# An FFN's first layer as seven products of quarters (Strassen) over blocks of 1024 tokens, in a fused gated block

## The chip, the core and the metric

The kernel runs on one core of a Trainium2 chip. The core has a matrix engine (TensorE, "PE" in the profile; its weight loads are listed apart as "PEld"), VectorE ("DVE"), ScalarE ("ACT"), GpSimd ("POOL") and an engine that here only issues transfers ("SP"). Each engine works through its own list of instructions in order; engines wait for one another by semaphores. The metric is the device time of one execution in microseconds (us). "Median" is over the runs shown.

## The reference

2048 tokens of 512 numbers go through two gated residual steps. All numbers are float32.

```python
# step 1: each token belongs to one of 4 experts, by its id; ctx[e] is 512 x 512
h = layernorm(x)
g = silu(h @ ctx[e].T)
u = h @ ctx[e].T                # the same matrix is used for gate, up and down
x = x + tanh(g_xattn) * ((g * u) @ ctx[e].T)    # e: the token's expert

# step 2: a dense FFN; its results are added up into 8 rows
xr = layernorm(x)
probs = softmax(xr @ wr.T)      # 8 routes
top2, idx = top_k(probs, 2)
gates = top2 / top2.sum()
h = silu(xr @ w1.T)
h = silu(h @ w3.T)
h = h @ w2.T
out = zeros_like(x)
for k in range(2):
    out[idx[:, k]] += gates[:, k] * h
x = x + tanh(g_ffn) * out
```

Since idx is at most 7, only rows 0 to 7 of `out` are not zero. The gated sum can so be taken before the last product with w2, over all tokens.

## The kernel before, in words

**Sorting.** Tokens are sorted by expert on the chip. They fill 17 "slots" of 128 rows: 13 slots of whole tiles of one expert (numbers 0 to NF - 1 = 12), and four "packed" slots (13 to 16, written NF to NF + 3) whose four groups of 32 rows can have different experts. A whole slot needs one matrix of 1 MB, a packed slot four. `from_row` and `to_row` hold, for each slot, which rows of x it reads and writes.

**One slot.** POOL gathers its rows (`gather`, an indirect transfer). DVE takes the mean off (`centre`: bn_stats, bn_aggr, subtract). TensorE transposes the tile into `tp_a` (`turn_in`), and ACT copies it to `hT`. TensorE multiplies it with the expert's matrix `m` into `z` (`up`); ACT makes g = silu(z), and DVE multiplies g by z. TensorE transposes g (`turn_mid`, `tp_g`), ACT copies it to `gT`, and TensorE multiplies with the same matrix into `y` (`down`). DVE adds y to x; POOL scatters the new rows to the output (an indirect transfer). DVE normalises them for the FFN (`norms`: bn_stats, an inverse root in nine small steps, together with that of a later slot's first norm). TensorE transposes the result (`turn_out`, `tp_f`), and ACT copies it into `hT2`, a block's input with tokens along the columns. For a packed slot ACT makes four copies, at column positions read from the table `first`.

**The main loop.** It is written out by hand as a software pipeline over `order`, the list of slots. Turn i does up(i), turn_in(i+1), centre(i+2), gather(i+3) and load(i+3), down(i-1), turn_out(i-2), norms(i-1), turn_mid(i). Here "slot i" in a turn means the i-th of `order`. TensorE's list in one turn is thus: z (four matmuls), tp_a, y (four matmuls), tp_f, tp_g. The order in which the code is written is the order on every engine: nothing is rescheduled.

**FFN work as filler.** `ffn(b)` is a generator over a block of 512 tokens. `step()` runs it up to its next `yield`, and is called twice in each turn. It becomes available when the last slot of its block has been through turn_out. Its parts are: four products `u` (L582; 128 columns of w1 each, all 512 tokens, four row chunks of 128 summed in one PSUM bank), each followed by a Silu on ACT into `s1`; the route logits `lg` (16 small products in groups of 32 columns), which DVE transposes and from which `route` makes the gates; four products `v` with w3, each followed by a Silu into `s2`; and four small products that add gate times s2 into `acc`. What is left when the loop ends runs as a tail with nothing beside it. In the last block the end is cut finer (`add_turned`, `finish`, `out_product`), and the 8 rows are written.

**Buffers.** The expert matrices rotate through eight buffers (`mp`), the x tiles through five (`xp`). PSUM has eight banks: four for products of all kinds (`ps_mm`), three for transposes (`ps_tp`), one for `acc`. A buffer is reused when its last reader is done. The instruction that fills it waits for that, and so does all that stands behind it on its engine or queue. SP's queue carries all loads of matrices and weights in the order of the code; POOL's queue carries gathers and scatters; ACT's and SP's carry the last stores.

**Start.** While the sort runs, TensorE does matmuls on constants (`busy`). ACT computes tanh of the two gates first; its first Silu is that of g of slot 0. The weights w1, wr, w3 and w2 are loaded behind the first matrices.

## Time and profile before

| | |
|---|---|
| median of 3 runs | 288.35 us (288.25 to 288.72) |
| the profiled execution | 287.71 us, of which 286.0 are the span from the first to the last instruction |
| TensorE busy | 275.3 us (96% of the span), granted clock 1.0 |
| DVE, ACT, POOL busy | 128.4, 63.9 and 38.9 us |
| products z, y (each 232 records) | 61.8 and 61.5 us busy |
| products u, v (128 and 136 records) | 57.1 and 57.3 us busy |
| transfers | 42.5 MB, 149 GB/s over the span; about 392 GB/s from 29 to 64 us |

All times below are of the profiled execution, from the start of its span. A float32 matmul instruction appears as two records. TensorE's records overlap, since ends are modelled, so its durations are best read from one start to the next. A line of the timeline gives start, duration, engine, line and operation, output and inputs, and in brackets the idle time before it and what ended that. A line of the groups gives the number of records, the busy time, the mean of one in ns, and the idle time before them.

### The profile page before, as it was taken

To read this page: it belongs to the slowest core of one execution; us is meant where nothing else is said; L and a number is where in the kernel's file an instruction comes from. 1 tells how busy PE (TensorE), PEld (TensorE's weight loads), DVE (VectorE), ACT (ScalarE), POOL (GpSimd) and SP (SyncE) were. 2 spreads that over 40 slices of the span, in tenths; PEclk is the share of its full clock that TensorE was granted. 3 is DMA by queue.
4 is the path that set the end of the run, shared out by engine and by line. 5 is a ranking of instruction groups with operands and counts; after the bars stand their busy time and mean duration, and the time that the engine had idled before them with its cause. 6 is when DMAs were issued, how large, how long until landed. Compare 5 with 4: busy or idle time off the path is not lost.

```text
span 286.0 us, 3546 instructions
## 1 busy us (share of the span) xinstructions
PE 275.3 (96%) x1189; PEld 128.2 (45%) x1189; DVE 128.4 (45%) x572; ACT 63.9 (22%) x122; POOL 38.9 (14%) x62
## 2 busy tenths in 40 slices
PE   4889999999999999999999999999999999999994
PEld 1444455544435444534444544444343454344463
DVE  5488868764617751608260775160543330001300
ACT  2032233122222222221222222222221121111120
POOL 5420122221111111111111111010110100000000
PEclk9999999999999999999999999999999999999999
DMA  0677999994614169513269614053100000000000
GB/s 1 206 272 264 395 392 390 390 391 176 220 37 174 52 226 398 220 39 138 82 198 386 242 54 183 0 184 143 39 0 37 13 0 1 0 0 2 0 1 2
DMA packets 20722, 42.54 MB, mean 149 GB/s; under 512 B 2143, under 2 KB 2207, under 8 KB 20704
## 3 DMA queue, kind: packets, MB, share of 16 engines
q1 hardware_dynamic: 17664, 33.66, 32.2%
q0 software_dynamic: 2720, 8.65, 8.3%
q8 instruction: 9, 0.15, 0.2%
q14 instruction: 9, 0.07, 0.1%
q10 hardware_dynamic: 320, 0.01, 0.1%
HBM read 38.10 MB, written 4.47 MB: 149 GB/s over the span
## 4 chain that ended last, share of the span: by engine, by line
PE 91%; DVE 4%; DMA 3%; issue 1%; ACT 0%; POOL 0%; DVEq 0%
PE y L448 21%; PE u L582 19%; PE v L609 19%; PE z L448 19%; PE tp_f L375 3%; PE tp_g L375 2%; PE tp_a L375 2%; DMA x<-in_x_dram,from_row 2%; PE acc L621 2%; PE lg L595 1%; DMA idt<-in_ids_dram 1%; PE accT L631 1%; PE o L685 0%; ACT hT L512 0%; PE tok L266 0%
## 5 line engine op out<-in xcount | busy, mean ns | idle before, releaser
L448 PE MATMUL z<-m,hT 128*32 128x512 f32 (+1 forms) x232 | 61.8, 595 | 0.2 <-ACT hT L423 0.2
L448 PE MATMUL y<-m,gT 128*32 128x512 f32 (+1 forms) x232 | 61.5, 594 | 0.0
L582 PE MATMUL u<-hT,w 128*128 128x512 f32 x128 | 57.1, 595 | 0.5 <-ACT hT L512 0.5
L609 PE MATMUL v<-w,s 128*128 128x512 f32 (+1 forms) x136 | 57.3, 570 | 0.0
L462 DVE SCALAR_TENSOR_TENSOR g<-z,rs_a,g 128x512 f32<-128x512 f32 x17 | 12.8, 750 | 61.5 <-ACT g L461 61.5
L448 PEld LDWEIGHTS z<-m,hT 128*32 128x32 f32 (+1 forms) x232 | 22.9, 146 | 30.7 <-issue 29.6
L609 PEld LDWEIGHTS v<-w,s 128*128 128x128 f32 x136 | 24.9, 190 | 25.5 <-issue 24.9
L582 PEld LDWEIGHTS u<-hT,w 128*128 128x128 f32 x128 | 23.4, 190 | 27.1 <-issue 26.2
L448 PEld LDWEIGHTS y<-m,gT 128*32 128x32 f32 (+1 forms) x232 | 22.5, 146 | 27.9 <-issue 27.9
L477 POOL DMA_INDIRECT out_dram<-x,to_row x17 | 17.2, 1010 | 109.8 <-DVE x L476 108.6
L384 POOL DMA_INDIRECT x<-in_x_dram,from_row x17 | 16.6, 978 | 73.5 <-issue 25.4
L476 DVE SCALAR_TENSOR_TENSOR x<-y,tg,x 128x512 f32<-128x512 f32 x17 | 12.7, 750 | 20.9 <-PE y L448 20.9
L461 ACT ACTIVATE g<-z,rs_a 128x512 f32<-128x512 f32 x17 | 11.7, 687 | 38.4 <-PE z L448 32.7
L589 ACT ACTIVATE s<-u 128x512 f32<-128x512 f32 x16 | 9.6, 597 | 47.2 <-PE u L582 47.2
L617 ACT ACTIVATE s<-v 128x512 f32<-128x512 f32 (+1 forms) x17 | 9.7, 572 | 41.3 <-PE v L609 41.3
L554 DVE STREAM_TRANSPOSE lt<-lg 128x128 f32<-128x128 f32 x4 | 1.3, 317 | 37.2 <-PE lg L595 37.2
L512 ACT COPY hT<-tp_f 128x512 f32<-128x512 f32 x13 | 7.6, 586 | 42.7 <-PE tp_f L375 42.7
L335 DVE BATCH_NORM_STATS2 st_a<-x 128x6 f32<-128x512 f32 x16 | 11.0, 686 | 5.3 <-DMA x<-in_x_dram,from_row 5.3
L375 PEld LDWEIGHTS tp_f<-ident,h_f 128*128 128x128 f32 x68 | 8.2, 141 | 10.2 <-issue 10.2
L335 DVE BATCH_NORM_STATS2 st_f<-x 128x6 f32<-128x512 f32 x17 | 11.8, 695 | 0.6
L375 PEld LDWEIGHTS tp_a<-ident,h_a 128*128 128x128 f32 x64 | 7.7, 141 | 9.5 <-issue 7.8
L375 PEld LDWEIGHTS tp_g<-ident,g 128*128 128x128 f32 x68 | 8.1, 141 | 7.6 <-issue 6.3
(139 smaller groups left out, 201.1 us busy)
## 6 DMA issues: line engine op xcount, KB each, us to landing
m<-in_ctxT_dram SPq DMA_DIRECT2D x29, 1024.0 KB
w<-in_w1T_dram SPq DMA_DIRECT2D x1, 1024.0 KB
w<-in_w3T_dram SPq DMA_DIRECT2D x1, 1024.0 KB
w<-in_w2T_dram SPq DMA_DIRECT2D x1, 1024.0 KB
x<-in_x_dram,from_row POOLq DMA_INDIRECT x17, 5.7
out_dram<-x,to_row POOLq DMA_INDIRECT x17, 5.8
wr<-in_wrT_dram SPq DMA_DIRECT2D x1, 64.0 KB
x_first<-out_dram SPq DMA_DIRECT2D x4, 4.0 KB
```

The lines of the kernel that those rows point to most:

```text
L335: nc.vector.bn_stats(st, xt)
L375: nc.tensor.transpose(tp[:, k * P : (k + 1) * P], h[:, k * P : (k + 1) * P], ident)
L384: nc.gpsimd.indirect_dma_start(out=xt, out_offset=None, in_=x, in_offset=bass.IndirectOffsetOnAxis(ap=from_row[:, p : p + 1], axis=0),)
L448: nc.tensor.matmul(out_ps[i * n : (i + 1) * n, :], lhs[:, k * P + i * n : k * P + (i + 1) * n], m[:, k, :], start=(k == 0), stop=(k == KC ...
L461: nc.scalar.activation(g, z, AF.Silu, scale=rs)
L462: nc.vector.scalar_tensor_tensor(g, z, rs, g, ALU.mult, ALU.mult)
L476: nc.vector.scalar_tensor_tensor(xt, y, tg[:, 0:1], xt, ALU.mult, ALU.add)
L477: nc.gpsimd.indirect_dma_start(out=out, out_offset=bass.IndirectOffsetOnAxis(ap=to_row[:, p : p + 1], axis=0), in_=xt, in_offset=None, bou ...
L582: nc.tensor.matmul(u, w1[:, k, m * P : (m + 1) * P], hT[:, k, 0:TB], start=(k == 0), stop=(k == KC - 1),)
L589: nc.scalar.activation(s1[:, m, :], u, AF.Silu)
L609: nc.tensor.matmul(v, s1[:, k, t * P : (t + 1) * P], w3[:, k, c0 : c0 + n], start=(k == 0), stop=(k == KC - 1),)
L617: nc.scalar.activation(s2, v, AF.Silu)
```

## The change

Blocks become 1024 tokens (two instead of four). The first layer of a block, the product of w1 and hT2, is cut into quarters: w1 into A11, A12, A21, A22 (256 x 256, as stored with the input rows first), hT2 into B11, B12, B21, B22 (256 rows x 512 tokens). In place of eight products of quarters there are seven, by Strassen's scheme in Winograd's form. Four sums of w1's quarters, S1 to S4, are made once on POOL in turn 4; four sums of the block's input, T1 to T4, on DVE once the block is complete. A product of quarters is four matmul instructions: two column chunks c, two row chunks each, summed in a PSUM bank. Some products add onto the bank X that an earlier one has left, after ACT has copied the earlier state out (`kept`: c1, u2, c7); others are joined by a DVE add that writes s1 before its Silu (`active` with `other`). Those Silu are issued one step later (`catch_up`).

The logits of both halves of a block are computed when it is complete, ahead of the sums, in the banks that X will take. A block's second layer is as before, over its two halves of 512 tokens.

PSUM is shared out anew: two banks for z, y, v and Z, two for X and the logits, one for Y, two for transposes, one for acc. The matrices have seven buffers instead of eight. `hT`, `gT` and `g` have two instead of three, `s2` four instead of five. The tables of the sort lie in a pool that is closed, whose place the FFN's new tiles take. In `order` the first packed slot moves from position 7 to 6. The loads of w3 and w2 move from ahead of the loop to the end of turn 7. A Silu of the gates is put ahead of their tanh.

```diff
     assert E == 4 and G == 4
-    TB = 512
+    TB = 1024
     NB = NT // TB
-    TT = TB // P
+    HB = TB // 2
+    TT = HB // P
+    assert NB == 2 and KC == 4
     const = ctx.enter_context(tc.tile_pool(name="const", bufs=1))
-    mp = ctx.enter_context(tc.tile_pool(name="mp", bufs=8))
-    hp = ctx.enter_context(tc.tile_pool(name="hp", bufs=2))
+    mp = ctx.enter_context(tc.tile_pool(name="mp", bufs=7))
     xp = ctx.enter_context(tc.tile_pool(name="xp", bufs=5))
     work = ctx.enter_context(tc.tile_pool(name="work", bufs=3))
-    s1p = ctx.enter_context(tc.tile_pool(name="s1p", bufs=2))
     small = ctx.enter_context(tc.tile_pool(name="small", bufs=4))
-    ps_mm = ctx.enter_context(tc.tile_pool(name="ps_mm", bufs=4, space=bass.MemoryType.PSUM))
-    ps_tp = ctx.enter_context(tc.tile_pool(name="ps_tp", bufs=3, space=bass.MemoryType.PSUM))
+    ps_mm = ctx.enter_context(tc.tile_pool(name="ps_mm", bufs=2, space=bass.MemoryType.PSUM))
+    ps_x = ctx.enter_context(tc.tile_pool(name="ps_x", bufs=2, space=bass.MemoryType.PSUM))
+    ps_y = ctx.enter_context(tc.tile_pool(name="ps_y", bufs=1, space=bass.MemoryType.PSUM))
+    ps_tp = ctx.enter_context(tc.tile_pool(name="ps_tp", bufs=2, space=bass.MemoryType.PSUM))
     ps_acc = ctx.enter_context(tc.tile_pool(name="ps_acc", bufs=1, space=bass.MemoryType.PSUM))
+    positions = ExitStack()
+    pos = positions.enter_context(tc.tile_pool(name="pos", bufs=1))
+    on_the_way = {
+        "lane", "atlane12", "atlane4", "passes", "what", "place", "over", "rank_in", "incl",
+        "keep", "cum", "hot", "before", "later", "stepped", "behind",
+    }
     def ct_(shape, dtype, name):
+        if name in on_the_way:
+            return pos.tile(list(shape), dtype, tag=name, name=name)
         return const.tile(list(shape), dtype, tag=name, name=name)
...
     tg = ct_([P, 2], F32, "tg")
+    nc.scalar.activation(tg, gates, AF.Silu)
     nc.scalar.activation(tg, gates, AF.Tanh)
...
-    hT2 = {NB - 1: ct_([P, KC, TB + Q], F32, "hT2")}
+    hT2 = [ct_([P, KC, TB + (Q if b == NB - 1 else 0)], F32, f"hT2_{b}") for b in range(NB)]
+    s1 = ct_([P, KC, TB], F32, "s1")
     acc = ps_acc.tile([P, D], F32, tag="acc", name="acc")
...
-    order = [0, 1, 2, 3, 4, 5, 6, NF, 7, 8, NF + 1, 9, 10, NF + 2, 11, 12, NF + 3]
+    order = [0, 1, 2, 3, 4, 5, NF, 6, 7, 8, NF + 1, 9, 10, NF + 2, 11, 12, NF + 3]
     assert sorted(order) == list(range(NP))
...
         if p < NF:
-            b = p // TT
-            if b not in hT2:
-                hT2[b] = hp.tile([P, KC, TB], F32, tag="hT2", name=f"hT2_{b}")
-            nc.scalar.copy(hT2[b][:, :, p % TT * P : (p % TT + 1) * P], tp)
+            b, t = divmod(p, TB // P)
+            nc.scalar.copy(hT2[b][:, :, t * P : (t + 1) * P], tp)
             return
...
-    def route(b, lg):
+    def route(b, lt):
...
-        lt = small.tile([P, TT, Q], F32, tag="lt", bufs=2, name=f"lt_{b}")
-        nc.vector.transpose(lt.rearrange("p t q -> p (t q)"), lg)
         l1 = lt[:, :, 0:NR]
...
-    def ffn(b):
-        hT = hT2.pop(b)
-        s1 = s1p.tile([P, KC, TB], F32, tag="s1", name=f"s1_{b}")
-        for m in range(KC):
-            u = ps_mm.tile([P, TB], F32, tag="mm", name=f"u_{b}_{m}")
-            for k in range(KC):
+    def sums_of_w1():
+        h = D // 2
+        a11, a12 = w1[:, 0:2, 0:h], w1[:, 2:4, 0:h]
+        a21, a22 = w1[:, 0:2, h:D], w1[:, 2:4, h:D]
+        ss = [ffp.tile([P, 2, h], F32, tag=f"S{i}", name=f"S{i}") for i in range(1, 5)]
+        nc.gpsimd.tensor_add(ss[0], a21, a22)
+        nc.gpsimd.tensor_sub(ss[1], ss[0], a11)
+        nc.gpsimd.tensor_sub(ss[2], a11, a21)
+        nc.gpsimd.tensor_sub(ss[3], a12, ss[1])
+        return a11, a12, a22, ss
+    def sums_of_hT(b):
+        lgs = [logits(b, half) for half in range(2)]
+        b11, b12 = hT2[b][:, 0:2, 0:HB], hT2[b][:, 0:2, HB:TB]
+        b21, b22 = hT2[b][:, 2:4, 0:HB], hT2[b][:, 2:4, HB:TB]
+        ts = [ffp.tile([P, 2, HB], F32, tag=f"T{i}", name=f"T{i}_{b}") for i in range(1, 5)]
+        nc.vector.tensor_sub(ts[0], b12, b11)
+        lts[b] = [turned(b, half, lg) for half, lg in enumerate(lgs)]
+        nc.vector.tensor_sub(ts[1], b22, ts[0])
+        nc.vector.tensor_sub(ts[2], b22, b12)
+        nc.vector.tensor_sub(ts[3], b21, ts[1])
+        return b11, b21, b22, ts
+    def first_layer(b):
+        a11, a12, a22, (sa1, sa2, sa3, sa4) = w1_sums
+        b11, b21, b22, (t1, t2, t3, t4) = hT_sums[b]
+        xs_, c1s, u2s, ys, c7s = {}, {}, {}, {}, {}
+        late = []
+        def product(out_ps, a, bb, c, start):
+            for k in range(2):
                 nc.tensor.matmul(
-                    u,
-                    w1[:, k, m * P : (m + 1) * P],
-                    hT[:, k, 0:TB],
-                    start=(k == 0),
-                    stop=(k == KC - 1),
+                    out_ps,
+                    a[:, k, c * P : (c + 1) * P],
+                    bb[:, k, :],
+                    start=start and k == 0,
+                    stop=k == 1,
+                    skip_group_check=True,
                 )
-            nc.scalar.activation(s1[:, m, :], u, AF.Silu)
-            yield
-        lg = ps_tp.tile([P, P], F32, tag="tp", name=f"lg_{b}")
+        def kept(ps, name, c):
+            t = ffp.tile([P, HB], F32, tag=name, name=f"{name}_{b}_{c}")
+            nc.scalar.copy(t, ps)
+            return t
+        def active(m, half, ps, other=None):
+            to = s1[:, m, half * HB : (half + 1) * HB]
+            if other is not None:
+                nc.vector.tensor_add(to, ps, other)
+                late.append(to)
+            else:
+                nc.scalar.activation(to, ps, AF.Silu)
+        def catch_up():
+            for to in late:
+                nc.scalar.activation(to, to, AF.Silu)
+            late.clear()
+        def p1(c):
+            xs_[c] = ps_x.tile([P, HB], F32, tag="x", name=f"X_{b}_{c}")
+            product(xs_[c], a11, b11, c, True)
+            c1s[c] = kept(xs_[c], "c1", c)
+        def p2(c):
+            z = ps_mm.tile([P, HB], F32, tag="mm", name=f"Z_{b}_{c}")
+            product(z, a12, b21, c, True)
+            active(c, 0, z, c1s.pop(c))
+        def p6(c):
+            product(xs_[c], sa2, t2, c, False)
+            u2s[c] = kept(xs_[c], "u2", c)
+        def p7(c):
+            ys[c] = ps_y.tile([P, HB], F32, tag="y", name=f"Y_{b}_{c}")
+            product(ys[c], sa3, t3, c, True)
+            c7s[c] = kept(ys[c], "c7", c)
+        def p5(c):
+            product(xs_[c], sa1, t1, c, False)
+            active(2 + c, 1, xs_[c], c7s.pop(c))
+        def p4(c):
+            product(ys[c], a22, t4, c, False)
+            active(2 + c, 0, ys.pop(c), u2s.pop(c))
+        def p3(c):
+            product(xs_[c], sa4, b22, c, False)
+            active(c, 1, xs_.pop(c))
+        todo = [
+            (p1, 0), (p2, 0), (p1, 1), (p2, 1), (p6, 0), (p7, 0), (p5, 0),
+            (p4, 0), (p3, 0), (p6, 1), (p7, 1), (p5, 1), (p4, 1), (p3, 1),
+        ]
+        for i, (f, c) in enumerate(todo):
+            f(c)
+            if i % 2 == 1:
+                yield
+                catch_up()
+    def logits(b, half):
+        lg = ps_x.tile([P, P], F32, tag="x", name=f"lg_{b}_{half}")
         for k in range(KC):
-            cols = hT[:, k, 0:TB].rearrange("p (t c) -> p t c", t=TT)
+            cols = hT2[b][:, k, half * HB : (half + 1) * HB].rearrange("p (t c) -> p t c", t=TT)
             for i in range(P // Q):
...
                 )
-        g = route(b, lg)
-        yield
+        return lg
+    def turned(b, half, lg):
+        lt = small.tile([P, TT, Q], F32, tag="lt", bufs=2, name=f"lt_{b}_{half}")
+        nc.vector.transpose(lt.rearrange("p t q -> p (t q)"), lg)
+        return lt
+    def ffn(b):
+        yield from first_layer(b)
+        for half in range(2):
+            yield from second_layer(2 * b + half, route(2 * b + half, lts[b][half]))
+    NH = 2 * NB
+    def second_layer(b, g):
+        c_b = b % 2 * HB
         def gated(t, half=None):
...
                     v,
-                    s1[:, k, t * P : (t + 1) * P],
+                    s1[:, k, c_b + t * P : c_b + (t + 1) * P],
                     w3[:, k, c0 : c0 + n],
...
                 )
-            s2 = work.tile([P, n], F32, tag="s2", bufs=5, name=f"s2_{b}_{t}_{c0}")
+            s2 = work.tile([P, n], F32, tag="s2", bufs=4, name=f"s2_{b}_{t}_{c0}")
             nc.scalar.activation(s2, v, AF.Silu)
...
                 start=(b == 0),
-                stop=(b == NB - 1 if t < TT - 2 else b == NB - 2),
+                stop=(b == NH - 1 if t < TT - 2 else b == NH - 2),
             )
...
         s2s = []
-        if b < NB - 1:
+        if b < NH - 1:
             for t in range(TT):
...
     SHORT = 1
-    last = {b: max(i for i, p in enumerate(order) if min(p // TT, NB - 1) == b) for b in range(NB)}
-    running = []
+    last = {b: max(i for i, p in enumerate(order) if min(p // (TB // P), NB - 1) == b) for b in range(NB)}
+    running, hT_sums, lts = [], {}, {}
...
     row_tables()
+    positions.close()
+    ffp = ctx.enter_context(tc.tile_pool(name="ffp", bufs=1))
     up(order[0], inside=lambda: turn_in(order[1]))
...
     load(order[4])
-    w3 = load_w(w3T, "w3")
-    w2 = load_w(w2T, "w2")
     for i in range(2, NP + 2):
...
         step()
-        running += [ffn(b) for b in range(NB) if last[b] == i - 2]
+        for b in range(NB):
+            if last[b] == i - 2:
+                hT_sums[b] = sums_of_hT(b)
+                running.append(ffn(b))
+        if i == 4:
+            w1_sums = sums_of_w1()
+        if i == 7:
+            w3 = load_w(w3T, "w3")
+            w2 = load_w(w2T, "w2")
         if i < NP:
             turn_mid(order[i])
-        step()
+        if last[0] != i - 2:
+            step()
     fetched = False
...
```

More of the change, by code (lines that the diff above doesn't have):

```diff
@@ L184, in tile_gated_moe_ffn @@
     nc.tensor.matmul(cnt[:, 1], before, hot, start=True, stop=True)
-    idle = ps_mm.tile([P, TB], F32, tag="mm", name="idle")
+    idle = ps_mm.tile([P, D], F32, tag="mm", name="idle")
     def busy(n):
         for _ in range(n):
-            nc.tensor.matmul(idle, ones, ones.unsqueeze(1).to_broadcast([P, TB // P, P]), start=True, stop=True)
+            nc.tensor.matmul(idle, ones, ones.unsqueeze(1).to_broadcast([P, D // P, P]), start=True, stop=True)
     busy(10)
@@ L403, in turn_in @@
         tp = transposed(hs.pop(p), f"a{p}")
-        hTs[p] = work.tile([P, KC * P], F32, tag="hT", name=f"hT_{p}")
+        hTs[p] = work.tile([P, KC * P], F32, tag="hT", bufs=2, name=f"hT_{p}")
         nc.scalar.copy(hTs[p], tp)
@@ L412, in first_in @@
         nc.vector.bn_aggr(mvs[p], st)
-        hTs[p] = work.tile([P, KC * P], F32, tag="hT", name=f"hT_{p}")
+        hTs[p] = work.tile([P, KC * P], F32, tag="hT", bufs=2, name=f"hT_{p}")
         n = D // 2
@@ L458, in up @@
         expert_product(z, hTs.pop(p), p, inside)
-        g = work.tile([P, D], F32, tag="g", name=f"g_{p}")
+        g = work.tile([P, D], F32, tag="g", bufs=2, name=f"g_{p}")
         rs = rss.pop(p)
@@ L466, in turn_mid @@
         tp = transposed(gs.pop(p), f"g{p}")
-        gT = work.tile([P, KC * P], F32, tag="gT", name=f"gT_{p}")
+        gT = work.tile([P, KC * P], F32, tag="gT", bufs=2, name=f"gT_{p}")
         nc.scalar.copy(gT, tp)
@@ L653, in ffn @@
             add(t, s2s[t])
-        a = work.tile([P, D], F32, tag="a", bufs=1, name="a")
+        a = work.tile([P, D], F32, tag="g", bufs=2, name="a")
         nc.scalar.copy(a, acc)
```

## The prediction

> **What bounds the kernel now.** I read the page first: the busy row and the clock row by slices, the chain that ended last, then the group of the first layer's products.
>
> ```profile
> PE   4889999999999999999999999999999999999994
> PEclk9999999999999999999999999999999999999999
> PE 91%; DVE 4%; DMA 3%; issue 1%; ACT 0%; POOL 0%; DVEq 0%
> L582 PE MATMUL u<-hT,w 128*128 128x512 f32 x128 | 57.1, 595 | 0.5 <-ACT hT L512 0.5
> ```
>
> TensorE is busy in every slice after the start, at full clock, and carries 91% of the chain. So work taken from TensorE shortens the run one for one, if no new wait appears. The view of TensorE's waits says how little slack it gives away now:
>
> ```profile
> PE u L582 <- ACT hT L512: 0.5, 2, 0.2
> PE tp_g L375 <- DVE g L462: 0.3, 1, 0.3
> ```
>
> The timeline of TensorE gives the price of a product. Ends are modelled, so I take start to start: from the first u to tp_g is 76.57 - 73.13 = 3.44 us for x8 records, which are four matmul instructions (each is recorded twice): 0.86 us each.
>
> ```profile
> 73.13 3.60 PE L582 MATMUL u<-hT,w 128*128 128x512 f32 x8
> 76.57 0.60 PE L375 MATMUL tp_g<-ident,g 128*128 128x128 f32 x4
> ...
> 212.44 0.60 PE L375 MATMUL tp_g<-ident,g 128*128 128x128 f32 x4
> 213.28 3.70 PE L582 MATMUL u<-hT,w 128*128 128x512 f32 x8 [0.24 <-ACT hT L512]
> ```
>
> The last two lines are one of the two u waits. A transpose group takes 0.44 to the next start (76.57 to 77.00), so u stood 213.28 - 212.88 = 0.40 us.
>
> **The part removed.** 64 instructions (128 records) become 7 products x 2 column chunks x 2 row chunks x 2 blocks = 56. 8 x 0.86 = -6.9 us, all on the path. Both u waits go: the first reader of the finished hT is now the second logits tile, and the first logits tile (1.0 us on TensorE) lies ahead of it, while the copy is ready 0.8 us after the transpose: 2 x -0.40 = -0.8. Logits stand back to back, and in block 1 right behind the acc products. Each detour to 32-column products costs 0.2 us (four u take 3.44 alone, and 13.93 for sixteen where lg follows, 0.2 over 4 x 3.44); about two and a half of four detours go: -0.5.
>
> **What it adds, and what hides it.**
>
> Turns of the main loop without FFN products. Block 0 is complete only in turn 10, so such turns reach from turn 2 to turn 10, not to turn 5. Stages by window: each took 8.17 to 8.19 us and TensorE was busy throughout; none costs anything by itself.
>
> ```profile
> 53.27:61.44 8.17, 8.17 (x30) 4.18 (x28) 5.34 (x26) 2.23 (x5) 1.99 (x2) 1.00 1.05 392
> ```
> (Columns: length, PE, PEld, DVE, ACT, POOL busy, clock, DMA share, GB/s.) But DMA is full there, so three supplies have to be followed.
>
> (a) Matrices, with seven buffers instead of eight. The tight place is slot 10 (NF+1): its four need the four that slot 6 frees when its y ends. Now the nearest case is slot 7: its y ends at 101.1 and frees four. In windows of 1 us (same columns) the transfers start after 102 and end at 115.1:
>
> ```profile
> 102.00:103.00 1.00, 1.00 (x4) 0.51 (x3) 0.93 (x3) 0.36 (x1) 0.67 (x1) 1.00 0.28 86
> 114.00:115.00 1.00, 1.00 (x4) 0.48 (x3) 0.93 (x3) 0.00 (x0) 0.00 (x0) 1.00 1.01 379
> 115.00:116.00 1.00, 1.00 (x4) 0.42 (x3) 0.33 (x1) 0.00 (x0) 0.00 (x0) 1.00 0.12 45
> ```
> That is 14.0 us from release to landing, a gather and a scatter included. TensorE reaches z of slot 10 after two transpose groups and two turns, 0.9 + 2 x 8.2 = 17.3 us. Slack 3.3 us, cost 0. The moved w3 and w2 are issued in turn 7 behind these four, on SP's queue, and v needs them in turn 14. Slot 11's matrix queues behind them: 14.0 + 3 x 2.7 (1.05 MB at 392 GB/s) = 22.1 us, plus 0.7 for x, against 17.3 + 10.4 (turn 10 with its logits) = 27.7. Cost 0.
>
> (b) POOL. Four sums of w1 (128x512) enter its queue in turn 4, ahead of the gather of slot 8, between these:
>
> ```profile
> 55.46 1.02 POOL L477 DMA_INDIRECT out_dram<-x,to_row  x1 [0.30 <-DVE w_f L360]
> 62.24 0.97 POOL L384 DMA_INDIRECT x<-in_x_dram,from_row  x1 [5.76 <-DVE h_a L396]
> ```
> POOL stands 5.76 us there. No two-input row of POOL exists; the nearest is the IOTA of 1536 elements, 1.83 us, so 0.6 us for 512: four make 2.4. The Trainium skill, GPSIMD Engine Reference, section 3.1, speaks against this placement: a two-input fp32 add is about twice as slow there as on VectorE, 4497 ns for 2048 elements. A quarter is 1.1; with a dispatch cost I estimate up to 1.3 each, 5.2 in all. I take the page's 1.1, since an iota reads no operand: 4.5 us. Both fit, so 0 in the sum by either; each us over 5.76 would delay slot 8's gather by as much, and use the slack of (c).
>
> (c) The ring of five x buffers. Gather i+3 waits for the scatter of slot i-2, and POOL issues the next scatter 1.27 us after a gather. Scatters at 46.41 and 55.46 were followed by their gathers at 54.19 and 62.24, 7.8 and 6.8 us later: a turn of 8.1 to 9.1 us, on average 0.4 longer than TensorE's 8.18. This falls back 2.0 us over turns 6 to 10. It is hidden: the last such turn had y end at 60.57 and h_f end at 65.81, and its transpose comes a turn later, at 68.75: slack 2.9 us. And w3 and w2 no longer load this stage, so I take 0.
>
> PSUM. Product tiles go from four to two, transposes from three to two. The next user of a y buffer comes after tp_f, tp_g, z, tp_a, 4.75 us; the latest reader of y finished at 62.37, 1.8 us after it. Slack 2.9. Tightest is turn 12, whose z takes the buffer of Z_0: DVE has first to pass the four T sums (1024 elements; by rows of 0.75 for 512, 1.5 each; by bn_stats, 0.69 for 512 of which the one-element rows make 0.15 fixed, 1.2), two logit transposes (0.32), g, centring, x and norms (6.5 us in all per turn). Counted from z of slot 10 (0), the sums end near 18.1, Z_0 is added at 25.4 at the latest I find, and z wants its tile at 25.9. Cost 0 to 1.5; I take 0.2.
>
> The tail, where nothing else fills TensorE. In block 1 the last tile's four copies end 2.24 us after its transpose started:
>
> ```profile
> 231.28 0.60 PE L375 MATMUL tp_f<-ident,h_f 128*128 128x128 f32 x4
> ...
> 233.25 0.27 ACT L524 COPY hT<-tp_f 128x128 f32 x1 [0.16 <-ACT hT L524]
> ```
> acc and the first logits cover these (0.5 + 1.0 + 1.0 = 2.5), the second logits end at 3.5; DVE needs 2.3 + 1.2 (T1) + 0.3 (transposed logits) + 0.1 before X_0 may take the logits' buffer: +0.3 (0 to 0.7, with T1 at 1.5). From there each product pair lasts 1.72 us and lies between the writer and the reader of each tile: a copy takes 0.2 + 0.59 (the copies of gT), an add 0.25 + 0.75. Without that cover eight such handovers would cost about 0.9 each, 7 us. Before the second layer, its fourth row chunk comes 2.6 us after the last product; two Silu need 0.2 + 0.6 + 0.6. Cost 0. ACT gains twelve copies (7 us on 64 busy), DVE eight sums and twelve adds (8 x 1.2 + 12 x 0.75 = 19 us on 128): neither becomes the bound. The new waits have this behind them: on ACT a caught-up Silu waits for its add, with the next product's copy and the next slot's g behind it (the next overwrite of that X waits for the copy, 1.7 us later); on DVE T1 waits for the hT copies, with the logit transposes behind it, for which X_0 waits (counted above).
>
> The early Silu. It puts the one table load at the start, and takes the load of 1.28 us at 19.82 away from g of slot 0, where TensorE waits 0.35 us. Rows of ACT and DVE:
>
> ```profile
> 19.82 1.28 ACT L461 ACT_TABLE_LOAD   x1
> 21.11 0.69 ACT L461 ACTIVATE g<-z,rs_a 128x512 f32<-128x512 f32 x1
> ...
> 22.07 0.17 DVE L319 TENSOR_SCALAR first<-psum 128x16 int32<-128x16 f32 x1
> 22.15 0.74 DVE L462 SCALAR_TENSOR_TENSOR g<-z,rs_a,g 128x512 f32<-128x512 f32 x1
> ```
> The Trainium skill, ScalarE: Activation LUTs, "What ACT_TABLE_LOAD costs", charges 1.28 us plus a drain of 1.38, 2.66 in all; here the activation follows at once, so the row gives 1.28. By either DVE reaches g only behind its table work, with no gap: 0.
>
> **The sum.** -6.9 - 0.8 - 0.5 + 0.2 + 0.3 = -7.7 us. The profiled execution took 287.71 (span 286.0 and 1.7 around it): 280.0. The median of the runs is 0.64 above it, 288.35, so I forecast 280.7.
>
> **Rivals.**
> 1. The gain is there, but one hand-over leaks: z of turn 12, late matrices at slot 10, or the x ring at turn 10. For: slacks of 0.5 to 3.3 us, with DMA full. Against: each is positive. A leak of 1 to 5 us gives 281.7 to 285.7, typically 283.5.
> 2. The x ring becomes the clock of turns 6 to 10, and the kernel is slower. Price: five turns longer by 1.27 + L - 8.18 each, less the slack of 2.9, where L is scatter to gather. It decides at L = 9.0 us (5 x 2.1 - 2.9 = 7.6, the whole gain). At L = 9.5 it is 13.0 - 2.9 - 7.7 = +2.4: 290.7. For: more bytes packed into consecutive turns. Against: L was 6.8 to 7.8 at 392 GB/s, and 5.5 (73.92 to 79.38) when lighter.
> 3. The products do not become cheaper: two-step groups cost their weight loads. For: the accumulation is half as long. Against: weight loads are 190 ns within records of 430 and already change with each instruction. If the eight handovers showed too, -7.7 + 7 gives 287.7, no change.
>
> **How the numbers follow.** As summed 0.70 (its own range 279.8 to 281.7); better than that 0.02; rival 1 0.17; rival 3 0.03; rival 2 and kin 0.08. A difference under 0.2% (0.6 us) can't be told from none here. Faster 0.88, same 0.03, slower 0.09. From 279.6 (sums without any added wait, -8.2, and a little) up to 284.8 the range takes in most of rival 1.
>
> **What would show it.** Right: 112 records in place of 128 at the same start-to-start time, no TensorE waits on DVE or ACT over 0.5 us in sum between turns 6 and 13, one table load, X_0 of block 1 waiting 0.3 on DVE. Wrong: TensorE waiting for a transfer of m (slot 10), for x or h of turns 6 to 10, or for a DVE add; sums on POOL over 1.4 us each.

## The result and the profile after

The changed kernel takes 284.24 us (median of 4 runs, 284.15 to 285.21) against 288.30 before (4 runs, 288.18 to 288.72): a ratio of 0.9864, 95% interval 0.9840 to 0.9888. It is faster, and the time lies inside the range. But of the 7.7 us that the sum promised about 4 arrived: the time is that of the first rival, a gain that leaks, not that of the case I held likeliest (280.7). The range was met because it was made to take in that rival. The profiled execution took 284.29 us, with a span of 282.6.

The page of the changed kernel: TensorE and its clock by slices, and the chain that ended last by engine.

```profile
PE   4978999999999999999999999999999999999994
PEclk9999999999999999999999999999999999999999
PE 87%; DVE 7%; DMA 3%; issue 1%; ACT 0%; ACTq 0%; POOL 0%; DVEq 0%
```

TensorE still sets the time, at full clock, but DVE's part of the chain went from 4% to 7%: by these rounded shares some 8 us more of the chain run over DVE (which isn't all lost time). The view of TensorE's waits names two places that the view of before doesn't have, and one without a releaser:

```profile
PE z L461 <- DVE pads L320: 1.9, 1, 1.9
...
PE tp_f L388 <- DVE h_f L513: 0.6, 1, 0.6
PE lg L703 <- issue: 0.3, 1, 0.3
```

The two `u` waits are gone, as predicted, and no transfer of m or x, no copy or add of the FFN is in that view. The products themselves are as cheap as they were summed. This is TensorE's timeline in block 1, where nothing else runs:

```profile
220.29 1.98 PE L626 MATMUL X<-hT,w 128*128 128x512 f32 x4
222.11 1.88 PE L626 MATMUL Z<-hT,w 128*128 128x512 f32 x4
223.83 1.88 PE L626 MATMUL X<-hT,w 128*128 128x512 f32 x4
...
242.71 1.88 PE L626 MATMUL X<-hT,S 128*128 128x512 f32 x4
244.43 5.74 PE L734 MATMUL v<-w,s 128*128 128x512 f32 x13
```

Start to start a pair takes 1.72 us, and 14 pairs 244.43 - 220.29 = 24.14. So the gain was made, and something else took back the 3.5 us between the forecast (280.7) and the median.

**The start.** The timeline of the changed kernel, DVE's and TensorE's rows by time, and below it the same two ends of the stretch in the kernel before:

```profile
17.27 0.69 DVE L348 BATCH_NORM_STATS2 st_a<-x 128x6 f32<-128x512 f32 x1 [1.85 <-DMA x<-in_x_dram,from_row]
...
21.94 0.18 DVE L317 SCALAR_TENSOR_TENSOR to_row<-tok,pad 128x17 int32<-128x17 f32 x1
...
22.22 2.81 PE L461 MATMUL z<-m,hT 128*128 128x512 f32 x6 [1.88 <-DVE pads L320]
...
26.61 3.60 PE L461 MATMUL y<-m,gT 128*128 128x512 f32 x8
```
```profile
16.34 0.69 DVE L335 BATCH_NORM_STATS2 st_a<-x 128x6 f32<-128x512 f32 x1 [1.18 <-DMA x<-in_x_dram,from_row]
...
24.85 3.60 PE L448 MATMUL y<-m,gT 128*128 128x512 f32 x8
```

z of the second slot stands for 1.88 us until DVE is done with `to_row`, the last reader of the PSUM tile `tok` (the view names `pads`, the next instruction, but `pads` doesn't read it). The tiles that rotate through `ps_mm` up to here are cnt, idle, tok, z of slot 0, z of slot 1. With four banks the fifth tile takes that of cnt, long free; with two it takes that of tok. DVE reads tok in its row tables, which stand behind the centring of the second slot, and this waits for a gather. What it costs is read over a stretch that doesn't contain the gather: from that centring (`st_a`) to y of the first slot it takes 26.61 - 17.27 = 9.34 us, and 24.85 - 16.34 = 8.51 before. So 0.83 is lost. That the gather landed 0.93 later in this execution than in the profiled one of before isn't put down to the change: its landing moved between 16.3 and 17.4 from kernel to kernel, and the kernel before with an early Silu had it at 17.34.

**Turn 5.** One window of the changed kernel, from z of a whole slot to the next z (length, then busy time of PE, PEld, DVE, ACT, POOL, clock, DMA share, GB/s):

```profile
55.02:64.28 9.26, 8.66 (x30) 4.09 (x28) 9.12 (x25) 2.56 (x5) 7.64 (x7) 1.00 0.52 178
```

It is 9.26 us long, where 8.28 are to be had (kernels without the cause, below), and DVE is busy 9.12 instead of the 5.34 of the window before. The same stretch in the timeline, POOL, DVE and TensorE by time:

```profile
56.46 1.83 DVE L369 SCALAR_TENSOR_TENSOR q_f<-r_f,v_f 128x1 f32<-128x1 f32 x1
56.97 1.30 POOL L589 TENSOR_TENSOR S<-w 128x512 f32<-128x512 f32 x1
58.22 0.21 DVE L369 SCALAR_TENSOR_TENSOR q_a<-r_a,v_a 128x1 f32<-128x1 f32 x1
58.35 1.27 POOL L590 TENSOR_TENSOR S<-S,w 128x512 f32<-128x512 f32 x1
...
58.78 0.85 DVE L375 TENSOR_TENSOR r_f<-r_f,w_f 128x1 f32<-128x1 f32 x1
...
59.57 1.27 POOL L591 TENSOR_TENSOR S<-w 128x512 f32<-128x512 f32 x1
59.66 1.19 DVE L377 SCALAR_TENSOR_TENSOR q_f<-r_f,v_f 128x1 f32<-128x1 f32 x1
60.78 1.30 DVE L377 SCALAR_TENSOR_TENSOR q_a<-r_a,v_a 128x1 f32<-128x1 f32 x1
60.79 1.27 POOL L592 TENSOR_TENSOR S<-w,S 128x512 f32<-128x512 f32 x1
...
62.38 0.54 DVE L513 TENSOR_SCALAR h_f<-x,mv_f,rs_f 128x512 f32<-128x512 f32 x1
...
63.06 0.63 PE L388 MATMUL tp_f<-ident,h_f 128*128 128x128 f32 x4 [0.57 <-DVE h_f L513]
```

Four of DVE's one-element instructions, 0.15 to 0.22 us elsewhere, take 1.83, 0.85, 1.19 and 1.30. Each has two tensors as inputs, and each ends within 0.02 us of the end of one of POOL's sums (58.27, 59.62, 60.84, 62.06). The first of them starts 0.51 us before the recorded start of its sum; why is not shown (starts on POOL are rough). In all six profiles with the sums on POOL four such rows stretch, and each ends within 0.04 us of a sum's end. Here they lose about 4.4 us together; h_f had some 3.4 to spare (where the cause is absent, below, it ends at 58.94, and tp_f starts at 62.29), so tp_f waits, and g of the next slot, behind h_f on DVE, makes tp_g wait after it.

**Turn 10.** TensorE's timeline at the two groups of logits of block 0:

```profile
105.61 2.44 PE L703 MATMUL lg<-hT,wr 128*32 128x128 f32 x62
108.35 0.38 PE L703 MATMUL lg<-hT,wr 128*32 128x128 f32 x2 [0.31 <-issue]
108.66 1.00 PE L388 MATMUL tp_g<-ident,g 128*128 128x128 f32 x4
109.49 3.60 PE L461 MATMUL z<-m,hT 128*128 128x512 f32 x8
```

From lg to z it takes 3.88 us. Two groups at 1.01 and a transpose group at 0.44 make 2.46, so 1.42 more than summed, with gaps that no semaphore explains.

The three make 0.83 + 0.98 + 1.42 = 3.23 us. They are read from the profiled execution, for which the sum gave 280.0 (280.7 was for the median), and which took 284.29: 4.29 more. With the 0.93 of the later gather that is 4.16 of the 4.29.

### The profile page after: what moved, and what is told of

It reads as the page before. It is cut to its first block, busy times and chain, and to the rows that moved or that the text cites. A ratio compares the mean times of both kernels' runs of the same rounds, so it can differ in the third digit from the quotient of the medians.

```text
span 282.6 us, 3568 instructions
## 1 busy us (share of the span) xinstructions
PE 270.3 (96%) x1173; PEld 126.3 (45%) x1173; DVE 149.0 (53%) x592; ACT 69.5 (25%) x134; POOL 44.3 (16%) x66
## 4 chain that ended last, share of the span: by engine, by line
PE 87%; DVE 7%; DMA 3%; issue 1%; ACT 0%; ACTq 0%; POOL 0%; DVEq 0%
PE y L461 20%; PE v L734 20%; PE z L461 19%; PE X L626 10%; PE Y L626 5%; PE tp_g L388 3%; PE tp_f L388 3%; PE Z L626 2%; PE tp_a L388 2%; DMA x<-in_x_dram,from_row 2%; PE acc L746 1%; DMA idt<-in_ids_dram 1%; PE lg L703 1%; DVE q_f L369 1%; PE accT L756 1%
## 5 line engine op out<-in xcount | busy, mean ns | idle before, releaser
L626 PE MATMUL X<-T,S 128*128 128x512 f32 x32 | 15.0, 592 | 0.0
L481 ACT COPY gT<-tp_g 128x512 f32<-128x512 f32 x17 | 10.0, 586 | 12.5 <-PE tp_g L388 12.4
L644 DVE TENSOR_TENSOR s<-X,c 128x512 f32<-128x512 f32 x4 | 2.8, 692 | 16.2 <-PE X L626 16.2
L388 PE MATMUL tp_f<-ident,h_f 128*128 128x128 f32 x68 | 10.5, 276 | 0.6 <-DVE h_f L513 0.6
L388 PE MATMUL tp_g<-ident,g 128*128 128x128 f32 x68 | 10.5, 275 | 0.2
```

The costliest lines, as they stand in the source:

```text
L388: nc.tensor.transpose(tp[:, k * P : (k + 1) * P], h[:, k * P : (k + 1) * P], ident)
L481: nc.scalar.copy(gT, tp)
L626: nc.tensor.matmul(out_ps, a[:, k, c * P : (c + 1) * P], bb[:, k, :], start=start and k == 0, stop=k == 1, skip_group_check=True,)
```

## Experiments

A theory for each leak, and a rival. Each run has its ratio to the kernel before on the same chip, with its 95% interval. The runs lie on several chips (the four from after_again to w_late on one), so kernels are best compared by ratio. Three stretches of the profiled execution are compared: **start**, from the second centring to the first y (before: 8.51); **turn 5**, from z to z; **pair**, from the first logits in turn 10 to the next z (2.46 from its parts).

| kernel | median us (runs: range) | ratio | start | turn 5 | pair |
|---|---|---|---|---|---|
| changed | 284.24 (4: 284.15 to 285.21) | 0.9864 [0.9840, 0.9888] | 9.34 | 9.26 | 3.88 |
| after_again | 283.60 (5: 282.40 to 283.99) | 0.9810 [0.9784, 0.9836] | 9.33 | 9.50 | 3.21 |
| tok_bank | 283.18 (5: 281.47 to 284.68) | 0.9824 [0.9798, 0.9851] | 8.50 | 9.55 | 2.37 |
| sums_dve | 282.68 (5: 281.50 to 283.25) | 0.9784 [0.9760, 0.9809] | 9.33 | 8.28 | 3.97 |
| w_late | 283.44 (5: 282.69 to 284.28) | 0.9831 [0.9810, 0.9852] | 9.33 | 9.34 | 2.89 |
| plain_products | 289.04 (22: 288.60 to 290.85) | 1.0026 [1.0015, 1.0037] | 9.36 | 9.01 | 2.38 |
| pool_copies | 281.98 (4: 281.79 to 282.36) | 0.9775 [0.9755, 0.9795] | 9.34 | 8.28 | 2.62 |
| logits_apart | 283.69 (5: 282.84 to 284.15) | 0.9829 [0.9809, 0.9849] | 9.33 | 9.29 | split |
| tok_sums_apart | 281.47 (5: 281.31 to 281.92) | 0.9763 [0.9746, 0.9780] | 8.50 | 8.27 | split |
| tok_sums | 282.36 (6: 280.52 to 283.12) | 0.9764 [0.9733, 0.9795] | 8.51 | 8.27 | 3.85 |
| tok_sums_mid | 281.13 (5: 281.01 to 281.44) | 0.9741 [0.9721, 0.9761] | 8.51 | 8.28 | split |
| tok_sums_mid_rows | 281.14 (5: 280.75 to 281.75) | 0.9734 [0.9714, 0.9754] | 8.51 | 8.28 | split |
| before_silu | 288.37 (20: 287.88 to 290.05) | 0.9998 [0.9986, 1.0011] | 8.49 | – | – |

**The changed kernel again**, as the measure for the others:

> The changed kernel once more, as the measure for its three variants. Theory: three places of its own eat 3.9 us of the gain, and they are systematic: z of slot 1 waits for DVE's row tables (about 1.9 us in TensorE's waits), tp_f of turn 5 waits for h_f (0.6), and the two logits products of turn 10 take 3.05 us from first start to tp_g instead of 2.0. Rival: they are accidents of one execution (transfers landing late). Then this profile shows them elsewhere or not at all. Time in either case 284.2, ratio to before 0.986.

All three losses came back (9.33, 9.50, 3.21), so they are no accident of one execution; the pair's size is the one that moves most.

**The start: another bank for tok.**

```diff
-    tok = ps_mm.tile([P, NP], F32, tag="mm", name="tok")
+    tok = ps_y.tile([P, NP], F32, tag="y", name="tok")
```

> Only tok moves, from the two banks of products to the bank of Y, which is free then. Theory A: z of slot 1 stood because its bank was that of tok, which DVE reads last in to_row. Then the wait of about 1.9 us on DVE is gone; g of slot 0 is set by DVE's table work as in the kernel before, so a wait of 0.3 to 0.6 for g comes back, and y of slot 0 starts about 2.7 us after DVE starts g instead of 3.5. Gain 0.8 us: 283.4. Rival B: z of slot 1 stood for its gathered rows, which landed 0.9 us later than before; then the wait stays under another name and the time stays 284.2.

Timeline of this kernel:

```profile
16.50 0.69 DVE L348 BATCH_NORM_STATS2 st_a<-x 128x6 f32<-128x512 f32 x1 [1.34 <-DMA x<-in_x_dram,from_row]
...
23.20 0.63 PE L388 MATMUL tp_g<-ident,g 128*128 128x128 f32 x4 [0.61 <-DVE g L475]
...
25.00 3.60 PE L461 MATMUL y<-m,gT 128*128 128x512 f32 x8
```

The wait of z is gone, the smaller one of tp_g for g, known from before, is back, and the start takes 8.50 us, as before. In the table the start is 8.49 to 8.51 in every kernel whose tok has a bank of its own or four to rotate in, and 9.33 to 9.36 in every other one: the cause and its price, 0.83, are shown. In the time it can't be told from after_again, since the executions of both scatter by 1.6 to 3.2 us.

**Turn 5: the sums on another engine.** Theory A: POOL's two-input instructions hold up those of DVE. Rival B: DVE's small instructions are late there for another reason, or POOL's mere activity delays them. The first run puts the sums on DVE, one per turn:

```diff
-        nc.gpsimd.tensor_add(ss[0], a21, a22)
-        nc.gpsimd.tensor_sub(ss[1], ss[0], a11)
-        nc.gpsimd.tensor_sub(ss[2], a11, a21)
-        nc.gpsimd.tensor_sub(ss[3], a12, ss[1])
-        return a11, a12, a22, ss
+        yield a11, a12, a22, ss
+        yield nc.vector.tensor_add(ss[0], a21, a22)
+        yield nc.vector.tensor_sub(ss[1], ss[0], a11)
+        yield nc.vector.tensor_sub(ss[2], a11, a21)
+        yield nc.vector.tensor_sub(ss[3], a12, ss[1])
...
-            w1_sums = sums_of_w1()
+            summing = sums_of_w1()
+            w1_sums = next(summing)
+        if 4 <= i < 8:
+            next(summing)
```

> The four sums of w1 go from POOL in turn 4 to DVE, one in each of turns 4 to 7 (0.69 us each). Theory A: while POOL adds two SBUF tensors, DVE's instructions with two SBUF inputs stand until the POOL instruction ends; four of them took 5.2 us in place of 0.8 and h_f came late. Then the rows of the inverse roots in turn 5's norms return to 0.22 us at most, TensorE's wait for h_f is gone, the turn takes 8.2 to 8.3 instead of 9.26 us: gain 1.0 us, 283.2. Rival B: h_f was late because gathers and DVE had drifted behind in the longer stretch without FFN work, and the sums were innocent; then a wait for h_f or x stays in turns 5 to 9 and the time is 284 or more, as DVE has 2.8 us more to do.

Turn 5 takes 8.28 us and the wait for h_f is gone. The median is 0.9 us lower than that of after_again, but the two ranges overlap; the gain is shown by the turn. This doesn't yet say whether POOL's work as such or its kind did it. The second run keeps that edit and gives POOL four instructions of the same size with one tensor as input, whose result nothing uses:

```diff
+            spare = ffp.tile([P, HB], F32, tag="c1", name="spare")
+            for r in range(4):
+                nc.gpsimd.tensor_scalar(spare, w1[:, r, :], 1.0, None, ALU.mult)
```

> The sums are on DVE as in sums_dve, but POOL does four operations of the same length with one SBUF input (128x512 times 1.0) where the sums stood; their result is not used. Theory A: DVE is held only when both engines read two tensors from SBUF. Then the rows of the inverse roots stay at 0.22 us and below, no wait of tp_f for h_f, time as sums_dve (282.7). Rival B: any long POOL operation holds DVE; then the same rows grow to 1 us and more and the wait of 0.6 to 0.9 comes back, 283.6.

Its timeline at the same place:

```profile
57.03 6.45 POOL L890 TENSOR_SCALAR spare<-w 128x512 f32<-128x512 f32 x4
...
57.74 0.22 DVE L377 SCALAR_TENSOR_TENSOR q_f<-r_f,v_f 128x1 f32<-128x1 f32 x1
57.88 0.22 DVE L377 SCALAR_TENSOR_TENSOR q_a<-r_a,v_a 128x1 f32<-128x1 f32 x1
...
58.40 0.54 DVE L513 TENSOR_SCALAR h_f<-x,mv_f,rs_f 128x512 f32<-128x512 f32 x1
...
62.29 0.60 PE L388 MATMUL tp_f<-ident,h_f 128*128 128x128 f32 x4
```

POOL is busy for longer than with the sums, and the two rows that took 1.19 and 1.30 us take 0.22; h_f starts at 58.40 instead of 62.38. Three DVE rows are longer than usual (the first q_f 0.58, the first sum 1.09 against 0.68 in sums_dve, h_a 0.67 against 0.49), which makes TensorE wait nowhere. So it isn't POOL's mere activity that made h_f late. Theory A holds, B falls. All six profiles with the sums on DVE have 8.27 or 8.28 in turn 5; all six with the sums on POOL have 9.01 to 9.55.

**Turn 10: what slows the pair of logits?** First theory: the heavy transfers at that time (387 GB/s from lg to tp_g), to which the later loads of w3 and w2 contribute.

```diff
-        if i == 7:
+        if i == 11:
```

> The loads of w3 and w2 go from the end of turn 7 to the end of turn 11, so the stretch around the logits of turn 10 has 2.1 MB less to carry before it. Theory A: TensorE's small logits products (128 records of 128 columns) ran dry of instructions, because instruction fetches share the transfer engines that the matrices kept full at 390 GB/s. With less traffic the pair takes 2.0 to 2.2 us instead of 3.05, and tp_g behind it 0.5: gain 1.0 to 1.3 us, 283.0. Rival B: two logits groups in a row are slow by themselves (in the tail, without traffic, the pair took 2.37); then the pair still takes about 3 us and the time stays 284.2.

A miss. The transfers were down to 162 GB/s during the logits, and the pair still took 2.89 us. And tok_bank, at 393 GB/s, had no gap at all:

```profile
104.30 1.95 PE L703 MATMUL lg<-hT,wr 128*32 128x128 f32 x64
106.18 0.66 PE L388 MATMUL tp_g<-ident,g 128*128 128x128 f32 x4
106.67 3.60 PE L461 MATMUL z<-m,hT 128*128 128x512 f32 x8
```

Second theory: it is the run of 32 small matmuls (64 records) in a row. The first half's group goes to turn 8, where its four slots are complete:

```diff
-        lgs = [logits(b, half) for half in range(2)]
+        lgs = [logits(b, half) for half in range(2) if half not in lts.get(b, {})]
...
+        if i == 8:
+            lts[0] = {0: turned(0, 0, logits(0, 0))}
```

> The logits of block 0's first half are made two turns earlier (turn 8), those of the second half stay in turn 10; everything else as in the changed kernel. Theory A: 64 records with their weight loads are more than TensorE's instruction supply gives in one burst, and the pair is slow for being a pair. Then each group takes 1.0 and the way from the second group's start to the next z is 1.6 us instead of 2.4 to 4.0 for the pair: gain 0.3 to 1.3, 282.9. Rival B: the supply is slow because transfers are dense there, whatever the burst; then the group of turn 10 alone still takes 1.5 to 2 us, and the time stays 283.6.

Timeline of this kernel:

```profile
106.32 0.60 PE L388 MATMUL tp_f<-ident,h_f 128*128 128x128 f32 x4
107.60 1.08 PE L703 MATMUL lg<-hT,wr 128*32 128x128 f32 x32 [0.68 <-ACT hT L523]
108.61 0.66 PE L388 MATMUL tp_g<-ident,g 128*128 128x128 f32 x4
```

A lone group takes 1.01 us, here and in turn 8. But the time isn't better than after_again: the second group now waits 0.68 us for ACT's copy of the last hT tile, the very wait that the first group had covered. The group in turn 8 (1.01), this wait (0.68), and the way from the second group to z (1.50) make 3.19 us, as much as the pair took in after_again (3.21). That explains the miss; the pair's gap itself is not explained. Groups alone had no gap in the four kernels that split them, pairs at turn 10 lost from nothing to 1.6 us over the same instructions (2.37 to 3.97).

What decides it stays open, but the traces narrow it. By the starts of the single records (the timeline joins them into rows), the five profiles that stop within the logits keep the pace of the others for 59 to 63 of the 64 records, and the first stop comes 1.66 or 1.67 us after the first start in each. In these five DVE's one-element steps of the inverse root have begun before that stop or begin within it (in the changed kernel v_f, the first of them, starts at 107.38, and TensorE stands from 107.27 to 107.62); in the three that don't stop (tok_bank, plain_products, pool_copies) they begin behind the last logits record (in tok_bank at 106.56, behind 105.98), and in pool_copies, where they begin with the transposes, these take 0.73 us against 0.49 in tok_bank. So the meeting with these steps separates the eight cases. It isn't shown to be the cause: no run moved the steps alone, in w_late the transposes ran beside them in 0.49, and the lone group of tok_sums_apart met them at its end (from 105.84) without a gap. Transfers of instructions are out: none was under way between lg and z in any of the eight.

**The product scheme alone.** Everything of the change is kept, but the seven products become eight ordinary ones of quarters (the sums are still made, and unused):

```diff
-        todo = [
-            (p1, 0), (p2, 0), (p1, 1), (p2, 1), (p6, 0), (p7, 0), (p5, 0),
-            (p4, 0), (p3, 0), (p6, 1), (p7, 1), (p5, 1), (p4, 1), (p3, 1),
-        ]
...
+        for m in range(KC):
+            for half in range(2):
...
+                    nc.tensor.matmul(
+                        u,
+                        w1[:, k, m * P : (m + 1) * P],
+                        hT2[b][:, k, half * HB : (half + 1) * HB],
...
+                active(m, half, u)
```

> The changed kernel with the first layer multiplied out in the ordinary way: eight products of quarters in place of seven (64 matmul instructions, one PSUM bank of four row chunks and a Silu each), everything else kept, the sums of w1 and of the input too, though nothing reads them. Theory: the seven products are worth what eight fewer instructions cost, 6.9 us on TensorE, and nothing of that is lost in the banks that are written twice. Then 290.5 (ratio about 1.007), slower than the kernel before by the waits that the rest of the change brought. Rival: half of the gain is lost in the hand-overs of X and Y; then the difference to the changed kernel is 3 to 4 us, 287.5.

289.04 us, 1.5 less than expected and 0.26% slower than the kernel before, an interval clear of 1. TensorE's timeline in block 1:

```profile
220.88 27.73 PE L690 MATMUL u<-hT,w 128*128 128x512 f32 x64
248.45 4.03 PE L738 MATMUL v<-w,s 128*128 128x512 f32 x9
```

27.57 us against 24.14: 3.43 in block 1, twice that 6.9, the predicted figure. The profiled executions differ by 288.67 - 284.29 = 4.38 only, since this one was luckier elsewhere: 1.50 in the pair, 0.25 in turn 5 and 0.56 in the landing of the gather, together 6.7. Without the saved products the rest of the change is thus a small loss.

**The early Silu alone**, in the kernel before:

```diff
     tg = ct_([P, 2], F32, "tg")
+    nc.scalar.activation(tg, gates, AF.Silu)
     nc.scalar.activation(tg, gates, AF.Tanh)
```

> The kernel before with the early Silu of the gates alone. As predicted: one table load instead of two, and no gain, since VectorE reaches g of slot 0 only behind its row tables: 288.4, ratio 0.999 to 1.001. Rival: the load of 1.28 us stands in the start's path, and the time falls by 0.35 us (the wait of TensorE there) or more, ratio 0.9988 or lower.

Ratio 0.9998 [0.9986, 1.0011]; the one table load is at 4.67 us, g's activation follows its copy without a second one, and nothing is won. A gain of 0.35 us (0.9988) lies just inside the interval, so the times alone don't exclude it; the start, 8.49 us, says that it isn't there.

**Leaks closed together.** tok's bank, the sums on DVE and the split logits:

> Three edits together: tok in Y's bank, the sums of w1 on DVE over turns 4 to 7, the logits of block 0 apart. If the three losses are separate and each is on the path, their gains add: 0.8 + 1.0 + 0.8 = 2.6 us under the changed kernel, 281.2, and the profile shows no wait of TensorE on DVE between turn 2 and the tail. If they hide one another (what is gained early is waited for later, on gathers or matrices), the time stays above 282.5 and a new wait on x, h or m appears.

281.47, 2.1 us under after_again, with intervals of the ratio that don't meet. The first two without the split:

> The changed kernel with two edits: the token tile in Y's bank, and the four sums of w1 on VectorE, one in each of turns 4 to 7. Block 0's two logits groups stay together at turn 10. If the two losses add, the sum is 283.6 - 0.4 - 0.9 to 1.4 = 281.5 to 282.3, with no wait of z for the row tables and none of the inverse root's transpose. Rival: the three-edit version gained chiefly by moving the logits, then this one stays near 282.7. The pair of logits groups is expected anywhere in 1.9 to 3.1 us, since neither of the theories so far has foretold it.

282.36, just above what was expected (up to 282.3), and from 280.52 to 283.12: in the profiled execution (283.12) the pair took 3.85 again. These two kernels differ in the pair alone; the one with the pair scatters by 2.6 us, the one without by 0.6. (pool_copies keeps the pair too, and its four executions scatter by 0.6 only.) Then the split with its new wait covered, by putting the second group and the T sums behind the middle of turn 10:

```diff
         if i < NP:
             turn_mid(order[i])
-        if last[0] != i - 2:
+        if last[0] == i - 2:
+            hT_sums[0] = sums_of_hT(0)
+            running.append(ffn(0))
+        else:
             step()
```

> As tok_sums, but block 0's first-half logits go to turn 8, and the second-half logits with the T sums stand behind the middle of turn 10, so that ScalarE's copy of the last hT tile lies behind TensorE's other work. Theory: the wait of 0.7 us for that copy goes, and nothing else comes: 281.5 - 0.7 = 280.8, about the forecast of 280.7. Rival: the T sums, later by a turn's half, make z of turn 12 or the first product of block 0 wait by 0.5 to 1.5 us, and the time stays at 281.5 or above.

Timeline of this kernel:

```profile
104.38 0.60 PE L388 MATMUL tp_g<-ident,g 128*128 128x128 f32 x4
105.22 1.08 PE L703 MATMUL lg<-hT,wr 128*32 128x128 f32 x32 [0.24 <-ACT hT L523]
106.23 3.70 PE L461 MATMUL z<-m,hT 128*128 128x512 f32 x8
```

The wait fell from 0.67 to 0.24 us, and the later T sums made no new one. 281.13 us, ratio 0.9741: inside the likeliest case's own range of 279.8 to 281.7 and 0.4 above its 280.7. It is faster than the kernel before and than the changed one (the ratio's interval ends at 0.9761, that of after_again begins at 0.9784). Last, the row tables behind g of the first slot:

```diff
+    up(order[0], inside=lambda: turn_in(order[1]))
     row_tables()
     positions.close()
     ffp = ctx.enter_context(tc.tile_pool(name="ffp", bufs=1))
-    up(order[0], inside=lambda: turn_in(order[1]))
```

> As tok_sums_mid, with the row tables behind the first slot's gate product on VectorE. Theory: g of slot 0 no longer stands behind the row tables, TensorE's wait of 0.5 us for it goes, 280.3. Rival: the row tables then hold up the scatter of slot 0, or the gather that needs them, and a wait for x appears in turns 1 to 3: 280.8 or more.

```profile
23.01 0.60 PE L388 MATMUL tp_g<-ident,g 128*128 128x128 f32 x4
...
25.45 0.63 PE L388 MATMUL tp_a<-ident,h_a 128*128 128x128 f32 x4 [0.98 <-DVE v_a L363]
```

281.14, no gain: tp_g no longer waits, but the tables now stand ahead of the third slot's centring, and tp_a waits for it instead. The start is 8.51 again; the wait only moved. The rival was right, with another victim than it named: DVE's whole list, not the place of one product, sets the start.

## Why the prediction was right and wrong

**Right: the sign, and the large term.** 112 records in place of 128 at the same 0.86 us an instruction: -6.9 predicted; 3.43 measured in block 1, twice that for two blocks. Both u waits went. X_0 of block 1 was to wait 0.3 us for the transposed logits, and its weight load waits 0.35 (the 2.37 us from the tail's logits to X_0 are two groups and this wait). The T sums take 1.18 to 1.23 us, as by the row that I chose. The eight hand-overs in the tail show no wait, z of turn 12 follows Z at once (the predicted 0.2 was 0), slot 10's matrices were in time, and the x ring, on which the slower case rested, never made TensorE wait. The early Silu is worth nothing. TensorE, not DVE or ACT, stayed the bound (DVE busy 149.0 us for 147 summed, ACT 69.5 for 71).

**Wrong by 0.98: the step "(b) POOL".** The duration was right (1.27 to 1.30 us, "up to 1.3 each"), and the four fit the 5.76 us. But I asked only what the sums would delay on POOL's own queue, and put "0 in the sum by either". What they delayed was DVE. The page I drew the price from, the Trainium skill's GPSIMD Engine Reference, says in its section 1 (Specifications) that POOL shares its SBUF interfaces with VectorE, with contention against DVE instructions with two SBUF inputs. The trace agrees for sums, and adds the price: 4.4 us of DVE's time for 5.1 of POOL's, against a slack of h_f of 3.4, which the step never worked out. Beside POOL instructions with one tensor input, of which the page's row makes no exception, the measured rows differ: the same small DVE rows took 0.22 us in pool_copies (though a sum of 128x512 took 1.09 instead of 0.68). Over the six profiles the loss in turn 5 is 0.73 to 1.27.

**Wrong by 0.83: the step "PSUM".** It followed the pool that went from four buffers to two through the steady turns, and called turn 12 the tightest place. The rotation has to be followed from its first tile. At the start the tile two back is not another product but tok, whose reader on DVE stands behind a wait for a transfer.

**Wrong by 1.42 in the profiled execution: the pair of logits**, costed at 1.0 us for each of its groups from a lone group in the trace. Between executions the pair takes 2.4 to 4.0 us with its transpose. With the other two leaks closed, the three kernels that split it scatter by 0.4 to 1.0 us, the one that keeps it by 2.6. Why TensorE stands there is open; the step took the cost of a group in a run of 16 for that of a run of 32. A further gain was forecast for this spot (-0.5 for saved detours), which at turn 10 went under in the gaps.

The rival with the right time was right for another reason than it gave: it looked for the leak at the hand-over of turn 12, at late matrices and in the x ring, where the slacks of 0.5 to 3.3 us all held.

## What to carry to other kernels

When a buffer pool is made smaller, write down its tiles in order from the first instruction of the program, and ask for each who reads the tile whose place it takes, and what that reader waits for. When work goes to an idle engine, check what it shares with the busy ones: here an idle POOL was no free place for two-input sums, although they fitted its gap. Work that is moved away may have been the cover of a wait (here 0.68 us for a copy): before moving a group, name what its time was hiding.

## What the runs showed of the hardware

- While POOL ran an add of two SBUF tensors of 128x512 (1.27 to 1.30 us), four DVE instructions with two tensor inputs stood until POOL's instruction had ended: 1.83, 0.85, 1.19 and 1.30 us for one element per partition (0.15 to 0.22 otherwise). DVE instructions with one tensor among them ran at 0.14 to 0.21 us. Beside POOL instructions with one tensor input (four in 6.45 us) two of these four took 0.22; a sum of 128x512 on DVE took 1.09 there instead of 0.68.
- A run of 32 small matmuls (128x32 weights, 64 records) in turn 10 took between 1.88 us and 3.10 in eight profiled executions, and the transpose group behind it 0.49 to 0.93, with idle times of 0.2 to 0.35 us that no semaphore ends. In the five that stopped, the first stop came 1.66 or 1.67 us after the first start, behind 59 to 63 records. Runs of 16 took 0.90 to 1.01, without a stop. The load on the transfers (162 to 393 GB/s) doesn't separate the cases; whether DVE's one-element steps meet the run's end does, and no run tests whether that is the cause.
